# Edge attention of a graph network: the turned one-hots from a code product in place of transposes

## The chip, the cores and the metric

The kernel runs on one core of a Trainium2 chip. The metric is the device time of one execution in microseconds (us). Five engines work side by side, each through its own queue in order: TensorE (PE; its weight loads are listed apart as PEld), VectorE (DVE), ScalarE (ACT), GpSimd (POOL) and SyncE (SP). They wait for each other through semaphores. A matrix product reads SBUF and writes a bank of PSUM, from which VectorE or ScalarE fetch it. GpSimd and SyncE start the transfers from and to the main memory.

## The reference

The network has four blocks, each a graph layer on 1250 nodes and 20000 edges followed by a feed-forward layer. The change touches the graph layer of the second block, an attention over edges, with the features `x` of the nodes (512 wide), four heads of 128 and four numbers per edge. Cut to what matters:

```python
h = (x @ W).reshape(n, 4, 128)
a_src = (h * att_src[None]).sum(-1)
a_dst = (h * att_dst[None]).sum(-1)
alpha = leaky_relu(a_src[src] + a_dst[dst] + a_edge, 0.2)   # one row per edge, four heads
amax = segment_max(alpha, dst, num_segments=n)
ex = exp(alpha - amax[dst])
denom = segment_sum(ex, dst, num_segments=n)
att = ex / (denom[dst] + 1e-16)
out = segment_sum(h[src] * att[:, :, None], dst, num_segments=n)
```

`src` and `dst` are the end nodes of an edge, and the edges come sorted by `dst`. Every node has a loop onto itself as well. A batch norm and a residual follow.

## The kernel before, in words

The nodes are in ten blocks of 125. Edges are in groups of 512, so that all edges of a group have their `dst` in one block; a group lies in SBUF as four tiles of 128 edges, an edge per partition. There is room for 50 groups; 46 are worked through in any case, and the last four lie behind a branch (`rest`) that is not taken with this data: each of the lines named here has run for 46 groups.

`edge_bits` (line 1582) runs once, much earlier, among the experts of the first block's feed-forward layer. It writes each edge's place within its block (0 to 124) as a code: `CD` has, for each edge, 7 columns with the bits, 7 with the complements, one column of ones, and 12 for the edge's scores (four heads, each as a sum of three bf16 pieces). `SEL` holds, per head, the matching codes of the nodes, scaled by a huge number, so that a product of codes is the score where edge and node match and hugely negative where they don't.

`l1_edges` (line 1632) is the edge loop. It goes over pairs of groups, 23 of them, and each step of the algorithm is a small function:

- `gathers` (GpSimd, L405): fetches the rows of `h` of the `src` nodes with their scores, four transfers a group, three pairs ahead;
- `onehot` (VectorE, L1666): a matrix of 512 edges by 125 nodes, f32, 1 where the edge ends in the node;
- `pieces` (VectorE, L1676 to L1683): the scores, cut into bf16 pieces, into `CD`;
- `coded` (TensorE, L1687, and a ScalarE copy, L1690): eight transposes of `CD` give `R`, the codes of the pair's edges, 27 rows by 1024 edges, bf16, in two buffers;
- `spread` (TensorE, L1700): four products of `R` with `SEL` put the scores of a group into a grid of nodes by edges, one PSUM bank per head;
- `maxima` (VectorE, L1709 to L1717): the largest score of each node in the group, and the running maximum;
- `turned` (TensorE, L1694, and a ScalarE copy, L1696): four transposes turn the group's one-hot to nodes by edges, `ohT`, through one PSUM bank `tr`;
- `fetched` (TensorE, L1728): products of `ohT` with the nodes' maxima give each edge its own node's values;
- `weights_of` (VectorE and ScalarE, L1734 to L1738): the exponentials `ex`;
- `scaled` (ScalarE, L1748) and `scaled_v` (VectorE, L1752): the gathered rows times `ex`;
- `summed` (TensorE, L1758): the one-hot times the scaled rows, eight f32 products a group, which the profile lists as sixteen records;
- `added` (VectorE, L1767): the sum onto the block's accumulator, with the old part scaled down.

The order of the work on TensorE, VectorE and ScalarE is written out by hand (`manual_schedule`); the other queues follow the data. In iteration i the loop sums pair i - 1, weighs and scales pair i, finds the maxima of pair i + 1 and codes pair i + 2. On TensorE an iteration runs: `spread` of the first group, `summed` of the first, `spread` of the second, `turned` of the first, `summed` of the second, `turned` of the second, `coded`, both `fetched`. Ahead of the loop the first two groups are gathered, made to one-hots and turned; the iteration i = -2 then makes and codes their pieces, group by group.

Of the kernel before, what the change touches and what calls it, by code (L numbers as in the profile page):

```python
# [9 lines left out]
F32 = mybir.dt.float32  # L10
F16 = mybir.dt.float16
BF16 = mybir.dt.bfloat16
# [3 lines left out]
AF = mybir.ActivationFunctionType  # L16
OP = mybir.AluOpType
# [6 lines left out]
P = 125  # L24
NT = N // P
EJ = E // P
GS = 512
# [9 lines left out]
class Net:  # L37
# [1544 lines left out]
    def edge_bits(self):  # L1582

        nc, ES, f = self.nc, self.ES, self.g1
        nh, nb = 4, 7
        C = 2.0 ** 100
        nr = f.nr = 2 * nb + 1


        CD = f.CD = f.p.tile([128, ST, nr + 3 * nh], BF16, name="g1cd")  # L1590
        SEL = f.SEL = f.p.tile([nr + 3 * nh, nh, P], BF16, name="g1sel")
        with ExitStack() as c3:
            r = self.pool(c3, "g1b")
            T = r.tile([128, nh, nr + 3 * nh], F32, name="g1t")
            xp = r.tile([128, 1], I32, name="g1xp0")
            d0 = r.tile([128, ST], F32, name="g1d0")

            for t in (T[0:1, 0, 0:1], xp[0:1, :], d0[0:1, 0:1]):
                nc.vector.tensor_copy(t, self.S1[0:1, 0, 0:1])
            nc.vector.tensor_scalar(d0, ES[:, :, 1], float(2 ** nb - 1), None, OP.min)  # L1600
            x = r.tile([128, ST], I32, name="g1x0")
            nc.vector.tensor_copy(x, d0)
            nc.vector.tensor_copy(xp, self.iota_p)
            nc.vector.memset(T, 0.0)
            nc.vector.memset(T[:, :, 2 * nb:nr], -float(nb) * C)
            for h in range(nh):
                for j in range(3):
                    o = nr + j * nh + h
                    nc.vector.memset(T[:, h, o:o + 1], 1.0)
            nc.vector.memset(CD[:, :, 2 * nb:nr], 1.0)  # L1610
            bt = r.tile([128, nb], F32, name="g1bt")
            xs = [x, r.tile([128, ST], I32, name="g1x1")]
            for b in range(nb):
                y = xs[1 - b % 2]
                nc.vector.tensor_scalar(y, x, 1, None, OP.logical_shift_right)
                nc.vector.scalar_tensor_tensor(CD[:, :, b], y, -2.0, x, OP.mult, OP.add)
                nc.vector.tensor_scalar(CD[:, :, nb + b], CD[:, :, b], -1.0, 1.0, OP.mult, OP.add)
                yp = r.tile([128, 1], I32, name=f"g1yp{b}")
                nc.vector.tensor_scalar(yp, xp, 1, None, OP.logical_shift_right)
                nc.vector.scalar_tensor_tensor(bt[:, b:b + 1], yp, -2.0, xp, OP.mult, OP.add)  # L1620
                x, xp = y, yp
            nc.vector.tensor_scalar(T[:, :, 0:nb], bt[:, None, :].to_broadcast([128, nh, nb]), C, None, OP.mult)
            nc.vector.tensor_scalar(T[:, :, nb:2 * nb], bt[:, None, :].to_broadcast([128, nh, nb]), -C, C,
                                    OP.mult, OP.add)
            for h in range(nh):
                ps = self.bank("g1sel_ps")
                nc.tensor.transpose(ps[:nr + 3 * nh, :P], T[:P, h, :], self.ident[:P, :P])
                nc.vector.tensor_copy(SEL[:, h, :], ps[:nr + 3 * nh, :P])
            identb = f.identb = f.p.tile([128, 128], BF16, name="g1id")
            nc.vector.tensor_copy(identb, self.ident)  # L1630

    def l1_edges(self, ctx):
# [4 lines left out]
        nc, tc, ES, SI, f = self.nc, self.tc, self.ES, self.SI, self.g1  # L1637
        nh, ch, nr = 4, 128, f.nr
        tw = nh * (ch + 1) + nh
        ACC, AM, AE, t1, CD, SEL, identb = f.ACC, f.AM, f.AE, f.t1, f.CD, f.SEL, f.identb  # L1640
        gq = self.pool(ctx, "g1g", bufs=8)
        q8 = self.pool(ctx, "g1h", bufs=8)
        q4 = self.pool(ctx, "g1p", bufs=4)
# [4 lines left out]
        tr = self.bank("oht_ps")  # L1648

        mg = mx[3][:, :16 * nh].rearrange("p (k h) -> p k h", k=8)  # L1650
        st, pr = {}, {}

        def gathers(g, after=False):
            G = gq.tile([128, 4, tw], F32, name="G")
            ix, o = SI, 4 * g
            if after:

                ix, o = q8.tile([128, 4], I32, name="ix"), 0
                nc.vector.tensor_copy(ix, SI[:, 4 * g:4 * g + 4])
            for k in range(4):  # L1660
                self.gather(G[:, k, :], t1, ix[:, o + k:o + k + 1])
            st[g] = {"G": G}

        def onehot(g):
            oh = st[g]["oh"] = q8.tile([128, 4, P], F32, name="oh")
            nc.vector.tensor_tensor(oh, self.iota[:, None, :P].to_broadcast([128, 4, P]),  # L1666
                                    ES[:, 4 * g:4 * g + 4, 1:2].to_broadcast([128, 4, P]), OP.is_equal)
# [22 lines left out]
            nc.scalar.copy(pr[i]["R"][:, j0 * GS:j1 * GS], pc[:nr + 3 * nh, j0 * GS:j1 * GS])  # L1690

        def turned(g):
            for k in range(4):
                nc.tensor.transpose(tr[:P, k * 128:(k + 1) * 128], st[g]["oh"][:, k, :], self.ident)  # L1694
            ohT = st[g]["ohT"] = q4.tile([P, GS], F32, name="ohT")
            nc.scalar.copy(ohT, tr[:P, :])  # L1696

        def spread(g):
            for h in range(nh):
# [72 lines left out]
        def at(f, i, *args):  # L1772
            if 0 <= i < NP:
                f(i, *args)

        def one(f, i, j, *args):
            if 0 <= i < NP:
                f(2 * i + j, *args)
# [22 lines left out]
        with self.tc.manual_schedule(engines={E.DVE, E.Activation, E.PE}):  # L1801
            for j in range(2):
                gathers(j)
                onehot(j)
                turned(j)
            for i in range(-2, NP + 1):


                at(weights_of, i)
                if i >= 0:  # L1810
                    one(spread, i + 1, 0)
                kv = 2 if i == NP - 1 else 1
                one(scaled, i, 0, range(kv, 4))
                if i >= 0:
                    one(maxima, i + 1, 0)
                if i in (-1, 0):
                    one(gathers, i + 3, 0, True)
                for k in range(kv):
                    one(scaled_v, i, 0, k)
                one(summed, i - 1, 0)  # L1820
                if i > 0:
                    one(gathers, i + 3, 0)
                one(spread, i + 1, 1)
                one(added, i - 1, 0)
                if i == NP - 1:
                    for k in range(2):
                        one(scaled_v, i, 1, k)
                else:
                    one(scaled, i, 1, range(0, 2))
                if i >= 0:  # L1830
                    one(turned, i + 1, 0)
                one(scaled, i, 1, range(2, 4))
                one(summed, i - 1, 1)
                if i > 0:
                    one(gathers, i + 3, 1)
                one(maxima, i + 1, 1)
                if i in (-1, 0):
                    one(gathers, i + 3, 1, True)
                if i == -1:
                    for j in range(2):  # L1840
                        one(onehot, i + 2, j)
                if i == -2:
                    for j in range(2):
                        at(pieces, i + 2, j, j + 1)
                        at(coded, i + 2, j, j + 1)
                        one(gathers, i + 3, j, True)
                        if j == 0:
                            one(spread, i + 2, 0)
                            one(maxima, i + 2, 0)
                else:  # L1850
                    at(pieces, i + 2, 0, 2)
                if i >= 0:
                    one(turned, i + 1, 1)
                if i > -2:
                    at(coded, i + 2)
                for j in range(2):
                    one(fetched, i + 1, j)
                at(lowered, i + 1)
                one(added, i - 1, 1)
                if i >= 0:  # L1860
                    for j in range(2):
                        one(onehot, i + 2, j)
# [468 lines left out]
```

## Time and profile before

| | us |
|---|---|
| median of three runs | 2755.53 |
| lowest and highest | 2744.45, 2759.66 |
| the profiled execution, its own time | 2749.04 |
| its span, first to last instruction | 2747.2 |
| TensorE busy | 2457.0 (89%) |
| VectorE busy | 1429.9 (52%) |
| ScalarE busy | 822.4 (30%) |
| granted TensorE clock, mean of the span | 0.918 |

The edge loop lies between about 815 and 1205 us; 19 whole iterations of it, from 879.24 to 1169.93 us, take 290.7 us, in which TensorE is busy for 276.3 us, VectorE for 244.0, ScalarE for 209.0 and GpSimd for 144.3, with a mean granted clock of 0.88. Busy times of different engines overlap. A line such as "L1694 PE MATMUL oht_ps<-ident,oh 128*125 128x128 f32 x4" means: line 1694, four products on TensorE into the tile `oht_ps`, with a weight of 128 by 125 and 128 rows of 128 numbers as the other operand. What stands in square brackets is how long the engine was idle before it, and whom it waited for. The granted clock is TensorE's, as a share of its full speed.

### The profile page before, as it was taken

The numbers are of one execution on the slowest core, as the hardware profiler recorded it, in microseconds if no ns is written. First come the engines' busy times: TensorE is split into PE (matmuls) and PEld (weight loads), VectorE is DVE, ScalarE is ACT, GpSimd is POOL, SyncE is SP. The second block draws the span as 40 slices with busy tenths as digits, with TensorE's granted clock in tenths as the row PEclk, the third lists the DMA queues.
The fourth block names the chain that finished last, engine by engine and source line by source line (L and its number), as shares of the span: only waits on it lengthen the run. The fifth ranks groups of instructions, "written<-read, shape, count | busy, mean of one in ns | idle before, by whom it ended". The sixth has DMA issues, their size and how long they took to land. (4 is left out here: it accounts for less than half of the span.)

```text
span 2747.2 us, 29741 instructions
## 1 busy us (share of the span) xinstructions
PE 2457.0 (89%) x10370; PEld 1551.7 (56%) x10370; DVE 1429.9 (52%) x3192; ACT 822.4 (30%) x1824; POOL 475.3 (17%) x540
## 2 busy tenths in 40 slices
PE   6899889999896999985698999999998899679986
PEld 3555689999844777755444454445544334355442
DVE  8766652100146878854358995378943554621000
ACT  4541111212124767742122441124311222211110
POOL 0012111211006545401200000000002011132211
PEclk9999679999996988995889999999999999889998
DMA  3112246666515545504832103110113102459996
GB/s 83 50 38 76 81 137 198 206 210 202 166 39 167 145 125 144 138 20 151 300 102 80 51 35 107 60 48 32 62 47 117 60 2 79 143 202 371 362 372 234
DMA packets 106745, 360.03 MB, mean 131 GB/s; under 512 B 34817, under 2 KB 39702, under 8 KB 84827
## 3 DMA queue, kind: packets, MB, share of 16 engines
q1 hardware_dynamic: 59867, 252.68, 26.1%
q0 software_dynamic: 44560, 100.92, 14.0%
q10 hardware_dynamic: 2160, 4.45, 0.5%
q8 instruction: 84, 1.38, 0.2%
q14 instruction: 74, 0.61, 0.1%
HBM read 328.36 MB, written 29.53 MB: 130 GB/s over the span
## 5 line engine op out<-in xcount | busy, mean ns | idle before, releaser
L1118 PE MATMUL g_acc<-g_e,g2hh 125*128 125x417 f32 (+1 forms) x960 | 345.1, 520 | 7.4 <-DVE g_e L1108 7.4
L1118 PEld LDWEIGHTS g_acc<-g_e,g2hh 125*128 125x128 f32 x960 | 183.1, 192 | 167.0 <-issue 157.4
L1560 PE MATMUL f_ps<-f3wd,f3ht 128*39 128x512 f32 (+1 forms) x704 | 177.5, 622 | 26.9 <-DMA f3wd<-in_L_ffn_W_down_dram 26.7
L1758 PE MATMUL ac_ps<-G,oh 128*125 128x258 f32 x736 | 198.8, 429 | 1.8 <-DVE g1acc L1767 1.5
L405 POOL DMA_INDIRECT G<-t,SI x160 | 156.2, 976 | 235.9 <-issue 99.8
L1748 ACT ACTIVATE G<-G,ex 128x129 f32<-128x129 f32 x632 | 190.2, 390 | 0.8
L1758 PEld LDWEIGHTS ac_ps<-G,oh 128*125 128x125 f32 x736 | 153.2, 214 | 45.9 <-issue 13.8
L541 PE MATMUL f_ps<-f0xgt,f0w 128*128 128x187 f32 x1024 | 168.6, 324 | 0.1
L552 PE MATMUL f_acc<-f0ht,f0w 128*128 128x187 f32 x1024 | 166.5, 324 | 0.0
L541 PEld LDWEIGHTS f_ps<-f0xgt,f0w 128*128 128x128 f32 x1024 | 165.3, 191 | 0.4 <-DVE f0xgt L102 0.3
L552 PEld LDWEIGHTS f_acc<-f0ht,f0w 128*128 128x128 f32 x1024 | 164.5, 191 | 0.3
L1102 DVE SCALAR_TENSOR_TENSOR g_e<-g_qb,g_a 125x1250 f32<-125x1250 f32 x80 | 120.7, 1519 | 68.6 <-DMA g_qb<-g_qd 61.0
L1566 DVE TENSOR_SCALAR f3y<-f_ps,f3k_wsel 39x512 f32<-39x512 f32 x32 | 24.0, 749 | 248.3 <-PE f_ps L1560 247.8
L1103 ACT ACTIVATE g_e<-g_e,g_a 125x1250 f32<-125x1250 f32 x80 | 106.3, 1335 | 137.4 <-DVE g_e L1102 137.2
L1074 PE MATMUL g_ps<-g22w,g2ht 128*125 128x512 f32 x320 | 138.0, 593 | 0.0
L221 PE MATMUL c_ps<-ohs,ohd 128*125 128x512 f16 (+1 forms) x552 | 108.7, 345 | 21.7 <-DVE ohd L212 13.2
L1045 DVE CUSTOM_DVE_ANT_0 g_junk<-g_mb,g_asb 125x1250 f32<-125x1250 bf16 x80 | 116.9, 1461 | 20.0 <-DMA g_asb<-g_as 14.9
L1560 PEld LDWEIGHTS f_ps<-f3wd,f3ht 128*39 128x39 f32 (+1 forms) x704 | 44.7, 120 | 142.9 <-issue 99.8
L1108 DVE SCALAR_TENSOR_TENSOR g_e<-g_e,CT 125x1250 f32<-125x1250 f32 x80 | 116.2, 1454 | 7.3 <-ACT g_e L1103 7.0
L1709 DVE TENSOR_REDUCE gm<-mx_ps 125x1 f32<-125x512 f32 x184 | 114.0, 682 | 3.7 <-PE mx_ps L1700 3.7
L569 DVE TENSOR_SCALAR f0y<-f_ps,f0xg,f0r 128x512 f32<-128x512 f32 (+1 forms) x16 | 12.2, 802 | 187.1 <-PE f_ps L567 187.1
L215 DVE TENSOR_SCALAR ohs<-iota,ES 128x1250 f16<-128x1250 f16 x184 | 89.3, 543 | 34.7 <-PE c_ps L221 31.8
(664 smaller groups left out, 3864.4 us busy)
## 6 DMA issues: line engine op xcount, KB each, us to landing
f3wd<-in_L_ffn_W_down_dram SPq DMA_DIRECT2D x64, 1280.0 KB
f0w<-in_L_ffn_w_dram SPq DMA_DIRECT2D x64, 1024.0 KB
f3wu<-in_L_ffn_W_up_dram SPq DMA_DIRECT2D x16, 1024.0 KB
f1w<-in_L_ffn_w_dram SPq DMA_DIRECT2D x13, 1024.0 KB
g_mb<-mbd POOLq DMA_DIRECT2D x40, 305.2 KB, 3.3
g_qb<-g_qd SPq DMA_DIRECT2D x16, 625.0 KB
f2tv<-in_L_ffn_tv_W_dram SPq DMA_DIRECT2D x16, 512.0 KB
wa_w<-in_L_gnn_WT_dram SPq DMA_DIRECT2D x6, 1024.0 KB
```

What stands on the lines that cost most here:

```text
L405: self.nc.gpsimd.indirect_dma_start(out=out, out_offset=None, in_=table, in_offset=bass.IndirectOffsetOnAxis(ap=idx, axis=0))
L541: nc.tensor.matmul(ps[:, :cap], lhsT=w[:, k, f * 128:(f + 1) * 128], rhs=xgt[e][:, k, :], start=k == 0, stop=k == 3)
L552: nc.tensor.matmul(acc[e][d][:, :cap], lhsT=w[:, f, d * 128:(d + 1) * 128], rhs=ht[e][:, 4 * c + f, :], start=c == 0 and f == 0, stop=c == ...
L1045: nc.vector.tensor_tensor_reduce(junk, mb, asb[h], 1.0, -3e38, OP.add, OP.max, accum_out=mx[:, i, h:h + 1])
L1074: nc.tensor.matmul(ps[:P, :], lhsT=HT[:, k, i * P:(i + 1) * P], rhs=ws[hf][k // 4][:, k % 4, :], start=k == 0, stop=k == kt - 1)
L1102: nc.vector.scalar_tensor_tensor(e, qb[h][0], A8[:, s, h:h + 1], qb[h][1], OP.add, OP.max)
L1108: nc.vector.scalar_tensor_tensor(e, e, 1.0, self.CT[:, s, :], OP.min, OP.mult)
L1118: nc.tensor.matmul(accs[h][f][c][:, :cn], lhsT=H[:, s, h * 256 + f * 128:h * 256 + (f + 1) * 128], rhs=e[:, c0:c0 + cn], start=s == 0, sto ...
L1560: nc.tensor.matmul(ps[64 * h:64 * h + k, :], lhsT=ht[g][:n, f, j * k:(j + 1) * k], rhs=ws[h][:n, f - f0, :], start=f == 0, stop=f == nf - 1)
L1709: nc.vector.tensor_reduce(gm[:, 0, h:h + 1], mx[h][:P, :], AX.X, OP.max)
L1748: nc.scalar.activation(gv[:, k, h], gv[:, k, h], AF.Copy, scale=ex[:, k, h:h + 1])
L1758: nc.tensor.matmul(ac[j][:P, 0:2 * (ch + 1)], lhsT=v["oh"][:, k, :], rhs=v["G"][:, k, j * 2 * (ch + 1):(j + 1) * 2 * (ch + 1)], start=k == ...
```

## The change

`edge_bits` makes one more matrix, `SAME`: for each node its bits and complements (each 0 or 1), -6 in the row of ones (1.0 - nb with nb = 7), and 0 in the twelve rows of the scores. The product of `SAME` with an edge's code is 1 where all seven bits match and 0 or less elsewhere, so that a Relu gives the one-hot, turned. `turned` makes this product for 512 edges at once, from the same `R` that `spread` reads, and ScalarE's copy becomes a Relu. Since `R` must be there first, the two calls ahead of the loop move into iteration -2, behind `coded`. All other calls stay where they are.

```diff
@@ edge_bits
+            SAME = f.SAME = f.p.tile([nr + 3 * nh, P], BF16, name="g1same")
+            O = r.tile([128, nr + 3 * nh], F32, name="g1o")
+            nc.vector.memset(O[:, nr:], 0.0)
+            nc.vector.tensor_scalar(O[:, :2 * nb], T[:, 0, :2 * nb], 1.0 / C, None, OP.mult)
+            nc.vector.memset(O[:, 2 * nb:nr], 1.0 - nb)
+            ps = self.bank("g1sel_ps")
+            nc.tensor.transpose(ps[:nr + 3 * nh, :P], O[:P, :], self.ident[:P, :P])
+            nc.vector.tensor_copy(SAME, ps[:nr + 3 * nh, :P])
@@ l1_edges
         def turned(g):
-            for k in range(4):
-                nc.tensor.transpose(tr[:P, k * 128:(k + 1) * 128], st[g]["oh"][:, k, :], self.ident)
+            nc.tensor.matmul(tr[:P, :], lhsT=SAME, rhs=pr[g // 2]["R"][:, g % 2 * GS:(g % 2 + 1) * GS],
+                             start=True, stop=True)
             ohT = st[g]["ohT"] = q4.tile([P, GS], F32, name="ohT")
-            nc.scalar.copy(ohT, tr[:P, :])
+            nc.scalar.activation(ohT, tr[:P, :], AF.Relu)
@@ ahead of the loop
             for j in range(2):
                 gathers(j)
                 onehot(j)
-                turned(j)
@@ in iteration -2, in the loop over both groups
                         if j == 0:
                             one(spread, i + 2, 0)
                             one(maxima, i + 2, 0)
+                        one(turned, i + 2, j)
```

## The prediction

> **What bounds the kernel now.** I went from the whole to the loop that is edited. The chain that ended last names only 22% of the span and none of the edge loop's lines, so it decides nothing here. I read the loop by itself: iterations are counted from one L1687 (the code transposes of `coded`) to the next, and 19 whole ones run from 879.24 to 1169.93 us: 290.7 us. First the groups of instructions inside 879.24 to 1169.93; the columns are busy us, mean ns, and idle time before with what ended it.
> ```profile
> L1758 PE MATMUL ac_ps<-G,oh 128*125 128x258 f32 x608 | 165.3, 432 | 0.0
> L1700 PE MATMUL mx_ps<-R,g1sel 27*125 27x512 bf16 x152 | 48.9, 438 | 0.2 <-DVE ex L1736 0.2
> L1694 PE MATMUL oht_ps<-ident,oh 128*125 128x128 f32 x152 | 24.7, 285 | 0.0
> L1687 PE MATMUL cd_ps<-g1id,g1cd 128*27 128x128 bf16 x153 | 12.0, 220 | 14.9 <-DVE g1cd L1683 14.9
> ```
> TensorE is busy 95% of this stretch (276.3 of 290.7 us), and yet once in every iteration it stands still ahead of L1687, 14.9 us in all, until VectorE has made the code pieces (L1683). `coded` comes directly after the second `turned`. Second, TensorE in order of time, for an iteration of 13.72 us and one of 16.73 us:
> ```profile
> 1142.12 0.62 PE L1687 MATMUL cd_ps<-g1id,g1cd 128*27 128x128 bf16 x8 [0.86 <-DVE g1cd L1683]
> 1145.68 3.75 PE L1758 MATMUL ac_ps<-G,oh 128*125 128x258 f32 x16
> 1150.37 0.70 PE L1694 MATMUL oht_ps<-ident,oh 128*125 128x128 f32 x4
> 1150.91 3.65 PE L1758 MATMUL ac_ps<-G,oh 128*125 128x258 f32 x16
> 1154.40 0.60 PE L1694 MATMUL oht_ps<-ident,oh 128*125 128x128 f32 x4
> ...
> 1001.28 0.62 PE L1687 MATMUL cd_ps<-g1id,g1cd 128*27 128x128 bf16 x8 [0.65 <-DVE g1cd L1683]
> 1005.57 6.22 PE L1758 MATMUL ac_ps<-G,oh 128*125 128x258 f32 x16
> ```
> The same sixteen sums take 3.75 us in one and 6.22 in the other. In the short iteration VectorE never waits: it is the bound, 13.7 us. In the long one VectorE waits for those sums (23.7 us over 12 waits at L1767), and they are slow because the granted clock is halved. Third, the clock: I cut the loop into stretches of 3.413 us counted from 27.58 us (the window length that "TensorE: Matmul & The Clock Gate", Part 1, gives); each of those I looked at is wholly at 1.00 or wholly at 0.50. L1758's own time in some of them (columns: stretch, its length, matmul busy, weight-load busy, clock, DMA share, GB/s):
> ```profile
> 966.25:969.66 3.41, 0.45 (x3) 0.04 (x1) 1.00 0.72 194
> 1017.45:1020.86 3.41, 0.00 (x0) 0.00 (x0) 1.00 0.77 220
> 1140.33:1143.74 3.41, 0.50 (x3) 0.09 (x1) 1.00 0.74 201
> 1143.74:1147.15 3.41, 1.47 (x7) 1.28 (x8) 1.00 0.74 223
> 1167.63:1171.05 3.42, 0.66 (x4) 0.22 (x2) 1.00 0.03 7
> 1171.05:1174.46 3.41, 0.98 (x5) 0.86 (x6) 1.00 0.00 0
> 1174.46:1177.87 3.41, 3.41 (x9) 2.65 (x8) 0.50 0.01 2
> ```
> After 966.25, 1017.45 and 1171.05 the next stretch is at half clock; after 1140.33, 1143.74 and 1167.63 it is not. So the clock falls after a stretch in which TensorE does too little real work, and that is the lull from the end of the second `summed` to the next one: `turned`, the wait, `coded`, `fetched` (tiny products), `spread` on 27 rows. It is 5.0 us long in the short iterations. The 19 iterations: 7 at full clock (mean 13.85 us), 4 with one slow stretch (15.04), 8 with two (16.70); 7 x 13.85 + 4 x 15.04 + 8 x 16.70 = 290.7.
>
> **The change, part by part.**
> *Four transposes become one product*, twice an iteration. At full clock, from the last `spread` product to the first sum the single records are 0.85 us apart (1150.06 to 1150.91). After: one step from product to product (0.22 us, from L1700) and one into the sums (0.31 us, as L1700 to L1694 now): 0.53. So the second `summed` ends 0.32 us sooner, and the second `turned` is some 0.2 shorter: 0.5 us an iteration. On the path that sets the end this is worth nothing: `coded` waits for L1683 anyway, and the idle before it grows by the same 0.5. Were that cover gone, it would be worth 19 x 0.5 = 10 us.
> *The matrix R* is read by `turned` as it is by `spread` beside it, an iteration after `coded` wrote it: no new wait. *Copy becomes Relu*: a Relu of 128x500 from PSUM took 0.68 us at L1366, against 0.58 for the copy here; 0.2 us an iteration on ScalarE, hidden because `ohT` was ready 0.58 us before `fetched` (1017.98 against 1018.56) and now comes 0.5 us earlier.
> *Start of the loop*: both `turned` move behind `coded`. The table load of 1.28 us, now at L1696 at 818.3, would sit before the first copy of R, and one product (0.43 us at half clock) before the next `spread`: 1.7 us late, of which VectorE's wait for gathered rows (1.04 us at 845.94) hides 1.04. The first gather is put down to an `ohT` copy that ends 822.15; if that is true it could gain up to 1 us. Between -1 and +0.7: I take +0.3. Queues of SP and POOL get nothing new.
> *Set-up* (five small VectorE instructions, a transpose): the four like it cost TensorE 0.45 us (543.98 to 544.43): 0.1.
>
> *The clock.* This is the part that moves time. Ending the sums sooner lengthens the lull from 5.0 to 5.3 us, and the transposes leave it. Add L1694's time in the stretches above: 0.60 at 966.25, 1140.33 and 1167.63, 0.00 at 1143.74, 1171.05 and 1017.45. The totals that keep the clock are 1.10, 1.26, 1.47; those that lose it 1.05, 0.98, 0.00. One line, about 1.07, divides them; on L1758 alone none does (0.98 loses, 0.50 keeps). So the row says that transposes count. The page says, in Part 4 ("PE-mode transpose"), that transposing doesn't count as busy in the same way. By the row: a dip stays away only if both stretches that share the lull reach 1.07, 2.14 together; at 1140.33 and 1143.74 they have 2.57. After the change 0.60 (transposes) and 0.32 (longer lull) go: 1.65. No place of the lull keeps the clock, so every iteration dips. By the page, L1758 alone must hold something like 0.47 in the first stretch; 0.50 - 0.32 = 0.18, so of the seven stretches that kept the clock (0.50 to 0.83) all below 0.8 fall too, though a different alignment might save one iteration in six, as now. The new product can't replace it: in 1034.51 to 1037.93 `spread` is busy for 0.77 us and the clock still falls, so 27 rows count for little.
> Cost of a dip in every iteration: 967.98 to 1049.58 is such a run (16.64, 16.66, 16.73, 16.72, 14.86: mean 16.32). It repeats itself, as each long one shifts the lull by about 0.36 us against five stretches (17.07) and the short one by 2.2, together one stretch. 19 x 16.32 = 310.1, against 290.7: **+19.4**. By the page, with one iteration of 13.71 saved after each such five: (81.61 + 13.71) / 6 = 15.9, x 19 = 302, +11.
>
> **Sum.** The profiled execution took 2749.04 (span 2747.2). 2749.0 + 19.4 + 0.3 + 0.1 = 2769. It had 7 iterations without a dip; the median shown, 2755.5, is 6.5 above it, about two of them fewer, and the three runs' spread (15 us) is five such iterations of 2.9. A loop that always dips doesn't depend on that luck, so I set 2769 beside the median: +0.5%.
>
> **Rivals.**
> *The gate keeps its mix.* If 27-row products count after all, or the threshold lies lower, nothing else is on the path: 2755 (2745 to 2762). For it: the margins at the threshold are 0.05 us. Against it: 1034.51, and the lull grows anyway.
> *A heavier dip.* If each iteration gets two slow stretches, 19 x 16.70 = 317.3: 2776; if a longer lull also slows the iterations before 879, some us more. For it: the lull ends in the wrong stretch more often. Against it: five stretches are longer than 16.70, so the alignment must slide.
> *The other side: the clock stays up.* If the gate counts the product of 512 columns fully and transposes as idleness, the dips shrink. Its place is the stretch ahead of each slow one; it decides where counted work passes the threshold there. All 12 dips gone would give 2749 - (4 x 1.2 + 8 x 2.9) = 2721, half of them 2735. Against it: `coded` and `fetched`, which fill the lull, are unchanged.
> *TensorE sets the pace* and the 0.5 us are gained: 2755 - 10 to 12 = 2744. Against it: 0.65 to 0.86 us of idle before L1687, even in the long iterations.
>
> **How the numbers follow.** A measurement of this kernel tells about 0.5% (13.8 us) from no change, so the bounds are 2741.8 and 2769.3. Always dipping 0.58, own range 2761 to 2777; a little over half of it lies above 2769.3 (0.32 slower, 0.26 same). Heavier dip 0.15 (slower). Mix kept or pace of TensorE 0.16 (0.14 same, 0.02 faster). Clock stays up 0.11 (0.10 faster, 0.01 same). Slower 0.47, same 0.41, faster 0.12. The range leaves out the risen clock and the top of the heavy dip: 2745 to 2778.
>
> **What would show it.** Right: all or nearly all iterations between L1687s at 15 or 16.7 us, idle before L1687 at full clock 1.1 to 1.4 instead of 0.86, no iteration of 13.7; L1758's mean above 432 ns; the loop's clock under 0.88; VectorE's wait at L1767 above 24 us. Wrong: iterations of 13.7 as often as before (the transposes didn't count), or TensorE with no idle before L1687, or VectorE's own work in an iteration no longer 13.7 us.

## The result and the profile after

The kernel after takes 2770.62 us (median of six runs, 2769.64 to 2782.83), the kernel before 2756.45 on the same chip (six runs, 2744.45 to 2761.56): a ratio of 1.0072 with a 95% interval of 1.0047 to 1.0097, slower by 0.5 to 1.0%. The forecast was 2769, with 2745 to 2778 as its range.

The profiled execution has a span of 2768.3 us, against 2747.2: 21.1 us more. Lines below the new matrix have moved by 9 or 10: `coded` is L1696, the product of `turned` L1703, its Relu L1706, `spread` L1710, `summed` L1768, `added` L1777. The 19 whole iterations now run from 878.73 to 1191.82 us: 313.1 us instead of 290.7, so 22.4 more. Ahead of them 0.5 us was won, behind them 0.8: 22.4 - 0.5 - 0.8 = 21.1. The whole difference lies in the loop.

The row of the 19 iterations of the kernel before, then of the kernel after (columns: stretch, its length, busy us of TensorE, its weight loads, VectorE, ScalarE and GpSimd with counts of instructions, granted clock, DMA share, GB/s):
```profile
879.25:1169.93 290.68, 276.26 (x1369) 211.35 (x1369) 243.97 (x742) 209.04 (x646) 144.29 (x148) 0.88 0.51 138
878.73:1191.82 313.09, 294.41 (x1254) 212.20 (x1254) 247.08 (x742) 210.02 (x646) 140.56 (x148) 0.81 0.47 128
```
TensorE issues six fewer products in an iteration (1254 records for 1369; one of these lies on the edge of the stretch) and is busy 18 us longer, at a loop clock of 0.81 instead of 0.88. The groups of the loop after, and the wait for its sums before and after (groups: busy us, mean ns, idle before; wait: us in total, times, longest):
```profile
L1768 PE MATMUL ac_ps<-G,oh 128*125 128x258 f32 x608 | 184.4, 469 | 0.0
L1710 PE MATMUL mx_ps<-R,g1sel 27*125 27x512 bf16 x152 | 54.1, 482 | 0.0
L1703 PE MATMUL oht_ps<-R,g1same 27*125 27x512 bf16 x38 | 15.2, 400 | 0.0
L1696 PE MATMUL cd_ps<-g1id,g1cd 128*27 128x128 bf16 x152 | 11.8, 220 | 18.6 <-DVE g1cd L1692 18.6
...
DVE g1acc L1767 <- PE ac_ps L1758: 23.7, 12, 2.7
DVE g1acc L1777 <- PE ac_ps L1768: 41.9, 19, 2.7
```
The same 608 records of the sums cost 19 us more, and VectorE waits for them in all 19 iterations, 41.9 us, where it had waited in 12 for 23.7. One iteration of the kernel after in order of time:
```profile
1140.21 0.42 PE L1703 MATMUL oht_ps<-R,g1same 27*125 27x512 bf16 x1
1141.64 0.62 PE L1696 MATMUL cd_ps<-g1id,g1cd 128*27 128x128 bf16 x8 [1.00 <-DVE g1cd L1692]
1142.19 2.56 PE L1738 MATMUL mx_ps<-mn,ohT 125*128 125x8 f32 x16
1144.68 1.96 PE L1710 MATMUL mx_ps<-R,g1sel 27*125 27x512 bf16 x4
1146.57 5.51 PE L1768 MATMUL ac_ps<-G,oh 128*125 128x258 f32 x16
1152.02 1.07 PE L1710 MATMUL mx_ps<-R,g1sel 27*125 27x512 bf16 x4
1152.93 0.37 PE L1703 MATMUL oht_ps<-R,g1same 27*125 27x512 bf16 x1
1153.23 3.75 PE L1768 MATMUL ac_ps<-G,oh 128*125 128x258 f32 x16
```
From the end of the second product of `turned` to the first sum TensorE does no large work; then 16 sums take 5.51 us, which take 3.75 at full clock. The sums' own time in stretches of 3.413 us says when the clock falls:
```profile
1136.53:1139.94 3.41, 3.41 (x16) 2.91 (x16) 1.00 0.51 129
1139.94:1143.36 3.42, 0.34 (x2) 0.00 (x0) 1.00 0.74 203
1143.36:1146.77 3.41, 0.20 (x1) 0.20 (x2) 0.50 0.75 221
1146.77:1150.18 3.41, 3.41 (x9) 2.63 (x10) 0.50 0.21 71
```
0.34 us of sums, and the next stretch is at half clock; so is the one after that, which follows a stretch with 0.20. Call a stretch at half clock slow. Of the 19 iterations, 16 have two slow stretches (mean 16.73 us), 3 have one (15.13) and none is free of them; before it was 8 (16.70), 4 (15.04) and 7 (13.85). An iteration of either kind takes nearly the same time in both kernels; what differs is the mix: the old lengths in the new mix, 3 x 15.04 + 16 x 16.70, give 312.3, which is 21.6 of the 22.4 us.

### The profile page after: what moved, and what is told of

Its sections match the earlier page's. It is cut to its first block, busy times and chain, and to the rows that moved or that the text cites. A ratio compares the mean times of both kernels' runs of the same rounds, so it can differ in the third digit from the quotient of the medians.

```text
span 2768.3 us, 29471 instructions
## 1 busy us (share of the span) xinstructions
PE 2471.4 (89%) x10233; PEld 1548.4 (56%) x10233; DVE 1432.9 (52%) x3196; ACT 823.5 (30%) x1824; POOL 472.2 (17%) x540
## 5 line engine op out<-in xcount | busy, mean ns | idle before, releaser
L1768 PE MATMUL ac_ps<-G,oh 128*125 128x258 f32 x736 | 219.4, 461 | 1.8 <-DVE g1acc L1777 1.5
L1768 PEld LDWEIGHTS ac_ps<-G,oh 128*125 128x125 f32 x736 | 166.2, 232 | 61.5 <-issue 16.0
```

The lines of the kernel that those rows point to most:

```text
L1768: nc.tensor.matmul(ac[j][:P, 0:2 * (ch + 1)], lhsT=v["oh"][:, k, :], rhs=v["G"][:, k, j * 2 * (ch + 1):(j + 1) * 2 * (ch + 1)], start=k == ...
```

## The experiments

Theory A is the prediction's: the clock falls after a stretch with too little large work, and the transposes of the second group were large work in the right place. Rivals (B or C in what was expected): it is the transposes of either group, or only the lull's length, or something else than the clock. A "fill" below is a run of idle products whose result nobody reads, written into the bank `tr`; no kernel leaves anything of the computation out.

**Two chips of another kind.** The first seven kernels ran on two chips on which the kernel before takes 2858.6 and 2856.1 us, 100 us more than on the first. In the trace of it there, all of this lies in the edge loop. Whether that is a property of these chips or a state they were in, the runs don't tell. Most of the seven say little of the prediction; the pair of fills with 128 and with 27 rows says more.

One group alone by transposes:
```diff
@@ turned(g): the first group by transposes (g % 2 == 0); the other kernel has g % 2 == 1
-            nc.tensor.matmul(tr[:P, :], lhsT=SAME, rhs=...)
+            if g % 2 == 0:
+                for k in range(4):
+                    nc.tensor.transpose(tr[:P, k * 128:(k + 1) * 128], st[g]["oh"][:, k, :], self.ident)
+            else:
+                nc.tensor.matmul(tr[:P, :], lhsT=SAME, rhs=...)
```


> The changed kernel with the first group of each pair turned by four transposes again, and only the second by the product. The second sums end as late as before, so the lull is as long as before (5.0 us), but no transposes stand in it. Theory A (the clock's gate counts work in stretches of 3.4 us, and transposes count): the two stretches around the lull hold 2.57 - 0.60 = 1.97 us of counted work, under the 2.14 that it takes, so every iteration still dips: none of 19 at 13.7 us, the loop at about 310, in all 2765 to 2775. Theory B (transposes don't count, only the lull's length matters): the mix of before comes back, about 7 of 19 iterations at 13.7 to 14.1, in all 2745 to 2762. Rival C (not the clock, but the product, the Relu or what reads R costs the time by itself): half of the loss goes, 2763.

> The other half: the first group of each pair turned by the product, the second by four transposes, so that the lull is 0.3 us longer than in the kernel before but has its transposes. Theory A: 2.57 - 0.32 = 2.25 us of counted work against 2.14, so some places of the lull keep the clock: 2 to 6 of 19 iterations without a dip, 2755 to 2766. Theory B: the longer lull alone makes nearly every iteration dip, as in the changed kernel: 2765 to 2775. Rival C: half of the loss goes, 2763.

Measured: 2840.65 us, a ratio to the kernel before there of 0.9948 (0.9929 to 0.9967), and 2857.38, 1.0005 (0.9992 to 1.0018). No theory had this: here the product for the second group is a gain. The second of these kernels, which leaves the transposes in the lull, was not run on a chip of the first kind, so that half of the test stays open.

Fills ahead of the second `turned`, in the kernel after (six products of 128 rows, or of 27) and in the kernel before (four of 128):
```diff
+        def fill(n, rows):
+            for _ in range(n):
+                nc.tensor.matmul(tr[:P, :], lhsT=self.iota[:rows, :P], rhs=self.iota[:rows, :GS], start=True, stop=True)
@@ the loop
+                if 0 <= i < NP - 1:
+                    fill(6, 128)
                 if i >= 0:
                     one(turned, i + 1, 1)
```


> The changed kernel with six products added ahead of the second turned in each iteration, 128 rows by 512 columns of fp16 each, about 0.22 us each, 1.3 us together, into the bank that the next product overwrites, so that their result is used by nobody. They fill the idle time before the code transposes. Theories A and B (the clock's gate): 1.65 + 1.3 = 2.95 us of counted work against 2.14 (the kernel before had 2.57), so at least as many iterations without a dip as before, 7 to 17 of 19: 2725 to 2757, though TensorE does 30 us more work. Rival C, and any theory in which TensorE's work or the product itself is the cost: no gain, 2770 to 2800.

> The same six added products, of the same duration and in the same place, but over 27 rows in place of 128, as the new product and the spreading ones have. If the gate counts rows (27 of 128 is 0.21: 1.65 + 0.27 = 1.92, under 2.14): every iteration dips, 2765 to 2778. If it counts the time that TensorE is occupied: as with 128 rows, 2725 to 2757. Rival C: 2770 to 2800.

> The kernel before (four transposes for each group) with four of the idle products of 128 rows (0.22 us each, 0.9 us together) ahead of the second turned, which fill the idle time before the code transposes. Theory A: 2.57 + 0.86 = 3.43 us of counted work in the two stretches around the lull, against 2.14, the most of all kernels tried; once the loop has found a place of the lull that keeps the clock it stays there (13.7 us is nearly four stretches, 13.65): 12 to 19 of 19 iterations without a dip on a chip like the first, 2725 to 2742; on the chip of 2858.6 a gain of 20 us or more over the kernel before. Rival C or TensorE as the bound: 0 to 20 us slower than the kernel before.

Measured: 2849.67 (0.9975, 0.9965 to 0.9985), 2857.99 (0.9999, 0.9989 to 1.0008) and 2855.15 (1.0003, 0.9993 to 1.0013). The gain that A expected of the fills with 128 rows, 20 us or more in the last kernel, did not come. But the 19 iterations with six fills of 128 rows and with six of 27 rows, on one and the same chip, differ in their clock:
```profile
882.59:1272.60 390.01, 311.61 (x1370) 222.82 (x1369) 249.91 (x742) 208.11 (x646) 140.28 (x148) 0.82 0.38 103
882.33:1272.13 389.80, 320.22 (x1369) 229.81 (x1369) 250.02 (x742) 208.43 (x646) 140.47 (x148) 0.75 0.38 103
```
The fills are equal in number, place and columns, and the loops in length. With 27 rows all 19 iterations have three slow stretches, with 128 rows 16 have two and 3 have three. This is the cleanest test of the rows: with nothing else changed, 128 of them count for the clock more than 27. It also shows that on these chips something other than the clock sets the pace, since iterations with two and with three slow stretches both take 20.5 us. (In the profiled executions, what the two kernels differ by lies behind the loop.) To see what sets it, both kernels ran again there, unchanged:

> The kernel before, unchanged, for a trace of it on the chip that runs the experiments: the first four ran on a chip where the kernel before takes 2858.6 us, 100 more than where the prediction was tried, all of it inside the edge loop, with iterations of 18.5 to 20.9 us that hold a wait of 3 to 5 us after the code transposes which no engine's work explains. Theory A (a dip of the clock costs more on that chip, and the rule by which it falls is the same): there the kernel before dips in nearly every iteration too (0 to 4 of 19 without), since a long iteration has another period and so another alignment; on a chip like the first, 5 to 8 of 19 without a dip, 2744 to 2762. Rival (the chip's wait has nothing to do with the clock): the wait stands in iterations at full clock as well.

> The changed kernel, unchanged, for the same purpose. Theory A: every iteration dips, on either chip. On the chip of 2858.6 that is what the kernel before does as well, so the loss is 0 to 5 us there: 2855 to 2865; on a chip like the first 2766 to 2776. Rival C (the product or the Relu costs the time by itself): 13 us of loss on either chip.

Measured: 2855.48 (1.0001, 0.9991 to 1.0011) for the kernel before, and 2832.61 for the kernel after: **0.9914 (0.9898 to 0.9931), faster**, in four executions. On such a chip the change gains nearly 1%, where A had expected a loss of 0 to 5 us and rival C one of 13. The kernel before there, TensorE and then ScalarE in order of time:
```profile
1028.21 0.60 PE L1694 MATMUL oht_ps<-ident,oh 128*125 128x128 f32 x4
1029.46 0.62 PE L1687 MATMUL cd_ps<-g1id,g1cd 128*27 128x128 bf16 x8 [0.65 <-DVE rest L1681]
1030.01 2.17 PE L1728 MATMUL mx_ps<-mn,ohT 125*128 125x8 f32 x16
1036.39 1.86 PE L1700 MATMUL mx_ps<-R,g1sel 27*125 27x512 bf16 x4 [4.22 <-ACT R L1690]
...
1035.34 1.00 ACT L1690 COPY R<-cd_ps 27x1024 bf16<-27x1024 bf16 x1 [5.91 <-remote]
```
The transposes of `coded` are recorded as over at 1030.08; ScalarE's copy of what they wrote starts at 1035.34, and the profile names none of the core's engines for its wait. The semaphore events of the trace show why it starts then: TensorE's own count, which stands for finished products, rises only at 1035.32. So the completion comes 5.2 us after the recorded end. On the first chip it comes 0.01 us after it, in every iteration of both kernels. (Ends of products are modelled in this profile: whether the products themselves ran late or only their completion, it can't tell.) The waits of the loop from 900 to 1160 us, of the kernel before there, and then one iteration of the kernel after there:
```profile
ACT R L1690 <- remote: 64.3, 11, 6.0
PE mx_ps L1700 <- ACT R L1690: 49.7, 12, 4.7
DVE ex L1734 <- remote: 37.6, 11, 3.6
```
```profile
1001.54 0.62 PE L1696 MATMUL cd_ps<-g1id,g1cd 128*27 128x128 bf16 x8 [1.00 <-DVE rest L1690]
1004.55 1.00 ACT L1699 COPY R<-cd_ps 27x1024 bf16<-27x1024 bf16 x1 [3.37 <-PE mx_ps L1738]
```
With the hold, iterations of the kernel before settle at 20.5 us, six stretches of 3.413, each with three slow ones; its loop takes 390.2 us. By the semaphore events the completion comes 5.2 to 5.5 us after the recorded end in 17 of its 19 iterations; in the kernel after some 2.3 us in most (2.4 in the one shown). There iterations lie between 18.4 and 20.9, and the loop takes 372.3. Why completions are held on some chips, and why the change shortens it, stays open.

**Fill and half change again.** The five kernels that follow ran on chips on which the kernel before takes 2754 to 2757 us, as on the first.

> The kernel after, with the first group's one-hots turned by transposes as before and only the second group's by the product. If the kernel before takes about 2756 us here: theory A (only work inside the lull counts, and the lull follows the second group) expects no gain over the kernel after, 2765 to 2778 us, no iteration under 14.5 us; theory B (the four transposes of either group keep the clock) expects 2745 to 2762 us with several iterations of 13.9 us. If the kernel before takes about 2856 us here: 2835 to 2845 us, as in the run of this kernel before.

Measured: 2772.28, 1.0067 (1.0046 to 1.0088), like the whole change; 15 iterations with two slow stretches, 4 with one, none free. As A expected: the first group's transposes stand between two runs of sums and are worth nothing there; what matters is the second group's. A longer lull is not the cause here: in most iterations `coded` starts 1.15 us after the second product of `turned`, and 1.24 to 1.45 us after the second group's transposes in the kernel before.

> The kernel after, with six products of a 128-row operand (nobody reads their result) ahead of the second group's turned product. If the kernel before takes about 2756 us on this chip: theory A (the clock falls because TensorE has too little counted work in the lull) expects 2725 to 2757 us, with most iterations of the edge loop near 13.9 us and a loop clock above 0.90; theory B (the fall has another cause, so idle work in the lull does not help) expects 2768 to 2785 us, iterations of 16.6 us, loop clock 0.81. If the kernel before takes about 2856 us here (TensorE's completions held back in every iteration): A and B both expect 2840 to 2855 us as in the run of this kernel before.

Measured: 2771.78, 1.0048 (1.0025 to 1.0072). A was wrong about its size: the total is B's, though three iterations of 13.9 to 14.0 us are back (six have one slow stretch, ten have two) and the loop's clock, 0.85, lies between the two. The row of its loop, two whole stretches of it with all engines, and TensorE in order of time across them:
```profile
885.83:1189.82 303.99, 303.89 (x1370) 218.72 (x1369) 247.25 (x742) 208.80 (x646) 140.63 (x148) 0.85 0.49 132
```
```profile
1015.16:1018.57 3.41, 3.41 (x29) 2.83 (x29) 3.11 (x10) 1.87 (x4) 2.52 (x3) 1.00 0.81 214
1018.57:1021.99 3.42, 3.42 (x9) 2.18 (x8) 3.24 (x9) 2.96 (x11) 0.95 (x1) 0.50 0.66 208
```
```profile
1013.83 1.46 PE L1710 MATMUL oht_ps<-iota 128*125 128x512 f16 x6
1015.22 0.43 PE L1703 MATMUL oht_ps<-R,g1same 27*125 27x512 bf16 x1
1015.58 0.62 PE L1696 MATMUL cd_ps<-g1id,g1cd 128*27 128x128 bf16 x8
1016.13 1.95 PE L1742 MATMUL mx_ps<-mn,ohT 125*128 125x8 f32 x16
1018.01 1.45 PE L1714 MATMUL mx_ps<-R,g1sel 27*125 27x512 bf16 x4
```
TensorE is recorded as busy through every hundredth of the stretch at 1015.16, and the clock falls all the same. (The ends of products are modelled, so the record can hide short gaps between them.) The Trainium skill, "TensorE: Matmul & The Clock Gate", section "HAM oscillation — how this bites in real kernels", gives as the rule that there be no idle gap over about 3.4 us; by that rule this kernel would not dip at all. What fills the stretch, but for the tail of the fill, is products of 27 rows, of 8 columns, and narrow transposes. How much large work does keep it? The sums alone (L1772) in two stretches that hold no fill, but all four products of a `spread` (1.17 us in each), with the stretch that follows each:
```profile
1049.29:1052.70 3.41, 1.30 (x6) 1.15 (x7) 1.00 0.75 209
1052.70:1056.11 3.41, 2.46 (x12) 1.77 (x10) 1.00 0.30 94
1062.94:1066.35 3.41, 1.09 (x5) 0.97 (x6) 1.00 0.78 206
1066.35:1069.77 3.42, 3.42 (x10) 2.65 (x9) 0.50 0.43 130
```
1.30 keeps the clock, 1.09 loses it. If a `spread` counted like sums, the threshold would be near 2.3, and the kernel before could not have kept its clock at 1140.33 with 0.50 us of sums, 0.60 of transposes, 0.55 of `coded` and no `spread`. Over the four kernels before, after, and these two, I took all 229 stretches between 880 and 1165 us that are at full clock and added up sums, one-hot transposes and fills, each record cut where the next begins: every one of the 63 after which the clock falls has 1.10 us or less, every one after which it stays has 0.94 or more. Between 0.94 and 1.10, the ones that keep it all hold the second group's transposes and those of `coded`; so no exact weight of a transpose comes out of this.

The fill had the right effect in the wrong place. It moves the start of the lull to its own end, and behind it stand `turned` 0.36, `coded` 0.55, `fetched` 1.88 and `spread` 1.1 us: 3.9 us that count for little, more than a stretch. That this is why the fill brings back three iterations and not more is argued here; the next kernels test it. It also lengthens a slow iteration from 16.7 to 17.0. Its loop is 304.0 us, 9.1 less than that of the kernel after; its profiled execution came to the loop 7.1 us later, 2.8 of this in the two iterations ahead, whose fills fall into slow stretches, and 4.3 before the first fill: to the `coded` ahead of it, the kernel after took 846.4 us in the run above and 850.7 in its run on another chip, this one 850.8.

**Rows of zeros.** If rows are what counts, `spread` and the product of `turned` can be made to count at no cost: `R`, `g1sel` and `g1same` get 128 rows, those added being zero in the weights.
```diff
-        SEL = f.SEL = f.p.tile([nr + 3 * nh, nh, P], BF16, name="g1sel")
+        SEL = f.SEL = f.p.tile([128, nh, P], BF16, name="g1sel")
+        nc.vector.memset(SEL, 0.0)
...
+        RR = [q1.tile([128, 2 * GS], BF16, name=f"R{j}") for j in range(2)]
+        for j in range(4):
+            nc.vector.tensor_copy(RR[j // 2][:, j % 2 * GS:(j % 2 + 1) * GS], self.iota[:, :GS])
...
-                pr[i]["R"] = q.tile([nr + 3 * nh, 2 * GS], BF16, name="R")
+                pr[i]["R"] = RR[i % 2]
```
(`SAME` in the same way; the copy into R writes its first 27 rows.) Once with a fill of five products besides, once alone, and once in the kernel before, with its transposes:

> The kernel after, with R, g1sel and g1same of 128 rows in place of 27 (the rows added are zero in g1sel and g1same, so the products are unchanged), and five products of a 128-row operand, whose result nobody reads, ahead of the second group's turned product. If the kernel before takes about 2756 us here: theory A (a stretch of 3.413 us keeps the clock when sums, transposes and other products of 128 rows fill about 1.1 us of it, and products of 27 rows count for nothing) expects that in no stretch of the edge loop too little is left, since turned and spread count now: periods of 13.8 to 14.2 us throughout, loop near 266 us, 2715 to 2735 us in all. Theory B (rows are not what counts, or rows of zero do not) expects the mixture of the filled kernel, 2758 to 2780 us. If the kernel before takes about 2856 us here: A makes the slow stretches fewer but not the held completions, 2815 to 2850 us; B 2840 to 2858 us.

> The kernel after with R, g1sel and g1same of 128 rows alone, no idle products. If the kernel before takes about 2756 us here: theory A expects that turned and spread count, so that only the idle us, coded and fetched (about 3.4 us) are poor: most iterations near 13.7 us, some with one slow stretch, 2718 to 2745 us. Theory B expects the kernel after again, 2765 to 2780 us, with no iteration under 14.5 us. If the kernel before takes about 2856 us here: A 2815 to 2840 us, B 2828 to 2838 us, which does not tell them apart.

> The kernel before (four transposes per group) with R and g1sel of 128 rows, the rows added zero in g1sel. If the kernel before takes about 2756 us here: theory A expects spread to count for the clock as in the padded kernel after, and the second group's transposes to count in part where the turned product stands there, with a shorter idle stretch ahead of coded: fewer slow stretches than in the kernel before and about as many as in the padded kernel after or fewer, 2728 to 2748 us. The rival (the padding helps only together with the product, for instance because it shortens something else) expects 2750 to 2762 us. If the kernel before takes about 2856 us here: A 2835 to 2856 us, the rival 2852 to 2860 us.

Measured against the kernel before on the same chips: padded and filled **2722.48 us, 0.9884 (0.9839 to 0.9930)**, in four executions; padded alone 2745.96, 0.9965 (0.9947 to 0.9984); the kernel before padded 2737.07, 0.9935 (0.9916 to 0.9954). The rows of their 19 iterations, in this order, one kernel to a fence:
```profile
879.99:1145.61 265.62, 257.07 (x1350) 192.59 (x1350) 242.38 (x742) 208.08 (x647) 142.32 (x148) 0.99 0.57 150
```
```profile
880.80:1171.31 290.51, 263.36 (x1254) 205.64 (x1255) 246.32 (x742) 209.25 (x646) 140.89 (x148) 0.86 0.52 138
```
```profile
879.75:1156.70 276.95, 253.96 (x1368) 206.19 (x1369) 244.37 (x742) 208.66 (x646) 141.87 (x148) 0.93 0.54 144
```
A's ranges were 2715 to 2735, 2718 to 2745 and 2728 to 2748; the second was missed by 1 us, the other two hold. Of the padded kernel after, A had expected most iterations near 13.7 us, and that was wrong: four are. An iteration of the padded and filled kernel:
```profile
1088.81 1.24 PE L1716 MATMUL oht_ps<-iota 128*125 128x512 f16 x5
1089.89 0.38 PE L1709 MATMUL oht_ps<-R,g1same 128*125 128x512 bf16 x1
1090.46 0.62 PE L1702 MATMUL cd_ps<-g1id,g1cd 128*27 128x128 bf16 x8 [0.19 <-DVE g1cd L1698]
1091.01 1.95 PE L1748 MATMUL mx_ps<-mn,ohT 125*128 125x8 f32 x16
1092.82 1.27 PE L1720 MATMUL mx_ps<-R,g1sel 128*125 128x512 bf16 x4
1093.92 3.65 PE L1778 MATMUL ac_ps<-G,oh 128*125 128x258 f32 x16
1097.41 1.02 PE L1720 MATMUL mx_ps<-R,g1sel 128*125 128x512 bf16 x4
```
The order is that of the filled kernel. Four products of `spread` take 1.02 us with 128 rows (1097.41), 1.07 with 27 (1152.02 above): the rows cost no time. But only `coded` and `fetched`, 2.4 us, are now poor, and seventeen of nineteen iterations have no slow stretch, 13.7 to 14.3 us each. In the two that do, the stretch ahead of the fall had 0.85 and 0.87 us of large work with `turned` and `spread` counted in; the poorest that kept the clock had 1.07. The padded kernel after, without the fill, has `coded`'s wait for VectorE in the lull; one of its stretches falls with 1.19 us by that count, the only one outside. The iterations of all kernels on chips of the first kind, by their slow stretches:

| kernel | none | one | two | the 19, us |
|---|---|---|---|---|
| before | 7 | 4 | 8 | 290.7 |
| after | 0 | 3 | 16 | 313.1 |
| after, first group by transposes | 0 | 4 | 15 | 310.4 |
| after, filled | 3 | 6 | 10 | 304.0 |
| after, padded | 4 | 7 | 8 | 290.5 |
| before, padded | 11 | 5 | 3 | 277.0 |
| after, padded and filled | 17 | 2 | 0 | 265.6 |

In its profiled execution the padded kernel after is no better in the loop than the profiled one of the kernel before; its gain of 0.35% shows in the times of all executions alone. (The profiled one of the kernel before is a quick one, 2749.04 us against a median of 2756.)

So three things are shown on chips of the first kind: 27-row products hardly count for the clock, 128-row ones do, zeros in the weights included; the loss of the kernel after is the clock's; and with the clock kept the change costs no time (iterations without a slow stretch take 13.86 us in the padded and filled kernel, 13.85 in the kernel before), but padding without it does as well as padding with it or better: 0.9935 and 0.9965, whose intervals touch. The kernel before with padding and a fill was not run, so it is open whether the change has any part in the 0.9884.

## Why the prediction was right

*TensorE's shortened work is worth nothing on the path.* Right. TensorE lost six products an iteration and the loop became longer. The idle ahead of `coded` was to grow by 0.5 us an iteration to 1.1 to 1.4; its mean grew from 0.78 to 0.98 (14.9 and 18.6 us over 19). In most iterations of 16.7 us it is 0.65 before (as at 1001.28) and 1.00 after, so 0.35 of the 0.5. That term was mis-sized without effect on the sum. The Relu costs ScalarE next to nothing: 0.60 us, where the copy took 0.59.

*Transposes count for the clock, and no place of the lull keeps it afterwards.* Right: no iteration without a slow stretch. The row's reading (+19.4) and that of the Trainium skill, "TensorE: Matmul & The Clock Gate", Part 4 (+11; transposes don't count as busy in the same way), were set against each other; 22.4 was measured. The kernel with only the second group's transposes removed has none free either, and 15 of 19 with two. The line at 1.07 us that was to divide the stretches is not exact: in the filled kernel 1.09 us of sums lost the clock.

*A run of dips costs 16.32 us an iteration.* 16.48 was measured (313.1 / 19), the term that was off: I took one short iteration in five from the run at 967.98; three in nineteen came. That is the 3.0 us between 19.4 and 22.4.

*Start of the loop* +0.3: inside its range, by two larger terms that nearly cancel. At 878.73 the kernel after is 0.5 us early, but it was so before the edge loop began: the last batch-norm activation ahead of it starts at 805.60 us instead of 806.17, which nothing here explains. The start itself thus cost next to nothing. The table load of 1.28 us does stand ahead of the first copy of R, at 830.23 us, and the first gather in question starts at 820.64 instead of 822.50, as it would if it had waited for the `ohT` copy: 1.3 us won beyond the 0.6. *Set-up* +0.1: not to be seen under those 0.6 us. Behind the loop 0.8 us were won, which no step explains either.

*The sum.* Between the two profiled executions 21.0 us were measured (2749.04 and 2770.08) and 19.8 forecast: 3.0 too little in the loop, some 1.7 too much for the rest, so the sum is closer than its terms, by luck.

*The median*, set equal to the sum because a loop that always dips doesn't depend on luck: 2769 against 2770.62. The reason given fails: the runs lie hardly closer together for it, 13 us apart instead of 17. What spreads them stays open.

*The rivals.* "The clock stays up" and "the gate keeps its mix" fell. "TensorE sets the pace" fell: the idle ahead of `coded` is still there in all 19 iterations. "A heavier dip" was half right, 16 of 19. What none of them foresaw is a chip of another kind, on which the same change is 0.9% faster; the forecast holds for the first kind only.

## What to carry to other kernels

Where a loop has a lull on TensorE, add up what is in each stretch of 3.413 us by kind of product, not by busy time: taking away work that is off the critical path can cost the clock, and a TensorE that is recorded as always busy can lose it. A contraction of few rows can be padded with zero rows at no time of its own; here that and a short fill turned 2757 us into 2722. And measure a change of 1% on more than one chip.

## What the runs showed of the hardware

- The clock falls with TensorE recorded as busy for the whole of a stretch (3.41 of 3.41 us at 1015.16), if that is filled with products of 27 rows, of 8 columns and narrow transposes; sums of 1.09 us in a stretch lost it and of 1.30 kept it.
- Six products of 128 rows in the place of six of 27, in every iteration on the same chip, raised the loop's clock from 0.75 to 0.82.
- Products with a moving operand of 128 rows, of which 101 meet zero weights, count as large work, and four of them took no longer (1.02 us) than four of 27 rows (1.07): with them alone the loop of the kernel before had 3 iterations with two slow stretches in place of 8.
- On two of the chips TensorE's completions of `coded` came late. In the kernel before, traced on one of them, they came 5.2 to 5.5 us after the products' recorded end in 17 of 19 iterations (0.01 us on the first chip); the 19 then took 390 us instead of 291, while what lies ahead of iteration -1 (847.5 us against 847.2) and behind the 19 (1575.9 against 1577.3) took the same time as elsewhere. No run here shows the cause.
